# First layer's score term: copied through DRAM to all partitions in place of four TensorE transposes, with the kept products in two buffers

## The chip, the cores and the metric

The kernel runs on one core of one Trainium2 chip. The metric is the device time of one execution in microseconds, median of several runs. The engines are called as in the profile: PE is TensorE's matmul, PEld its weight load, DVE is VectorE, ACT is ScalarE, POOL is GpSimd, and SP is SyncE, whose queue (SPq) issues all DMAs of this kernel.

## What is computed

Two layers of graph attention over `x` of 64 batches x 256 nodes x 512 features, all float32. Each layer normalizes, clips at zero, attends along one 256 x 256 adjacency matrix, and adds to its input. The reference, cut to what matters:

```python
h = maximum(layernorm(x), 0)                       # layer 0
hw = h @ W                                         # 512 -> 256
e = (hw @ a[0]) + swapaxes(hw @ a[1], 1, 2)        # one term along rows, one along columns
alpha = softmax(leaky_relu(e, 0.2) + NEG * (1 - adj))
x = x + concatenate([alpha @ hw, hw], -1)

h = maximum(layernorm(x), 0)                       # layer 1: 8 heads of 64
q, k, v = h @ Wq.T + bq, h @ Wk.T + bk, h @ Wv.T + bv
attn = softmax(where(adj == 0, -inf, q k^T / 8))
x = x + (attn @ v) @ Wo.T + bo
```

In layer 0 the score of two nodes is a sum of two numbers, one for each node. The kernel holds the scores turned, with the attended node on the partitions, so one term is a number for each partition (a bias of the activation) and the other must lie along the free axis, the same on all 128 partitions. The change is about how that second term gets to all partitions.

## The kernel before, in words

A group is two batches, so there are 32 groups of 512 tokens, each in four row tiles of 128 (GT = 4). The program is unrolled; nothing loops on the chip. The main loop (lines 886 to 923) works on three groups at once: attention and output of group g (`scores`, `mask_pairs`, `weigh`, `outputs`), q, k and v of group g + 1 (`project`), and the first layer of group g + 2 (`first_layer`), with the first normalization of group g + 3 (`first_norm`) in between. These parts are generators, and two hand-written strings, `steps`, one for each batch of the group, say which of them goes on next: S is the scores, m a mask step, u a product of `project`, s a piece of `first_layer`, n a piece of `first_norm`, o an output product. PE's order is fixed to the order in which the program was written (`in_order`, line 131). Operations marked `not_sooner` stay behind their engine's last one; for the rest, the framework's scheduler chooses each engine's order when the program is built, and the engine then runs in that order. In the same way SP issues its DMAs in one fixed order, and each waits for its own semaphores while those behind it stand.

`first_layer(g)` (line 536): four products `ph` of the normalized input with W, to which two columns are joined that hold W a[1] and W a[0]. So H, 258 columns of them copied from PSUM by ACT, holds the score terms in its columns 0 and 1 and the product from column 2 on. Then `pn` (lines 551 to 553): column 0 of each of the four row tiles, read 128 times over, is transposed on PE against the identity. That leaves the 512 numbers along the free axis on every partition, in one PSUM bank. ACT then forms the scores `e` of both batches, 128 x 256 at a time, from `pn` and the bias in H's column 1; DVE does the leaky ReLU in place; ACT the exponential; and later, DVE the mask. `po` (line 577) multiplies `e` by H, and DVE divides and adds (`ri`, `x`).

`scores` (line 718): eight `sc` products of one batch, a PSUM bank each, with ACT's exponential into `p` (256 keys x 256 queries for 8 heads). `weigh` (line 754): the sums over keys (`total`), DVE's reciprocals `r`, the weighted values `pr`, and DVE's `oT` = pr times r. The `o_sums` and `sums` are operands of a seven-product scheme of matrix multiplication; `project` makes its seven products in two held banks and one turning bank. ACT copies three intermediate results out, the kept products (`kept`, line 683), to which DVE adds later products.

PSUM has five turning banks (`mm`, line 109), which `ph`, `pn`, `total`, `pr`, `sc`, `po`, second products of `project`, and products of `outputs` take in turn, and three held ones. `xt`, `passed` and `moved` (lines 443 to 462) are the normalized tiles on their way through DVE's 32 x 32 transpose and DRAM into `hT`, which is the transposed operand for the products; `passed` is stored by one DMA and `moved` fetched by four.

Of the kernel before, what the change touches and what calls it, by code (L numbers as in the profile page):

```python
# [8 lines left out]
F32 = mybir.dt.float32  # L9
I32 = mybir.dt.int32  # L10
# [4 lines left out]
P = 128  # L15
# [42 lines left out]
def bounded(  # L58
# [23 lines left out]
    nc = tc.nc  # L82
# [3 lines left out]
    B, N, D = x.shape  # L86
# [3 lines left out]
    NT = N // P  # L90
    GB = 2
    GT = GB * NT
    TOK = GB * N
# [8 lines left out]
    att = ctx.enter_context(tc.tile_pool(name="att", bufs=2))  # L102
    small = ctx.enter_context(tc.tile_pool(name="small", bufs=6))
    psum = ctx.enter_context(tc.tile_pool(name="psum", bufs=1, space=bass.MemoryType.PSUM))
    dram = ctx.enter_context(tc.tile_pool(name="dram", bufs=4, space=bass.MemoryType.DRAM))
# [3 lines left out]
    def mm(name):  # L109
        return psum.tile([P, 512], F32, tag="turn", name=name, bufs=5)  # L110
# [12 lines left out]
    def not_sooner(engine, operation, *args, **kwargs):  # L123

        last = engine.last
        after(getattr(engine, operation)(*args, **kwargs), last)
# [4 lines left out]
    def in_order(instruction):  # L131
        if before:
            after(instruction, before.pop())
        before.append(instruction.ins.name)

    def matmul(*args, **kwargs):
        in_order(nc.tensor.matmul(*args, **kwargs))  # L137

    def transpose(*args):
        in_order(nc.tensor.transpose(*args))  # L140
# [17 lines left out]
    ident = const.tile([P, P], F32, name="ident")  # L158
# [7 lines left out]

    w0_sb = const.tile([P, HP, F1 + 2], F32, name="w0_sb")
    nc.sync.dma_start(w0_sb[:, :, 2:], w0.rearrange("(c p) o -> p c o", p=P))
    adj_i = att.tile([P, NT, N], I32, tag="kept", name="adj_i", bufs=3)
    nc.sync.dma_start(adj_i, adj.rearrange("(t p) k -> p t k", p=P))  # L170

    def score_columns():
# [6 lines left out]
                )  # L179

    def mask():
        edge = att.tile([P, NT, N], F32, tag="kept", name="edge", bufs=3)
        not_sooner(vector, "tensor_scalar", edge, adj_i, 0.0, None, op0=ALU.not_equal)
        yield
        pt = mm("pt_mask").rearrange("p (k q) -> p k q", k=NT)
        for kb in range(NT):
            for t in range(NT):
                transpose(
                    pt[:, kb, t * P : (t + 1) * P], edge[:, t, kb * P : (kb + 1) * P], ident
                )  # L190
        not_sooner(vector, "tensor_copy", maskT, pt)

        not_sooner(vector, "reduce_max", bad[:, 0, :], edge, axis=AX.X)
        vector.tensor_scalar(bad[:, 0, :], bad[:, 0, :], 0.0, None, op0=ALU.is_equal)
        vector.tensor_tensor(edge, edge, adj_i, op=ALU.not_equal)
        vector.reduce_max(bad[:, 1, :], edge, axis=AX.X)
        yield
# [63 lines left out]
    def last_bias():  # L261


        wide = att.tile([P, 2, 2, P], F32, tag="kept", name="bv_wide", bufs=3)
        for q in range(NQ):
            for half in range(2):
                gpsimd.tensor_scalar(
                    wide[:, half, q, :], square_ones, bv_col[:, half, q : q + 1], None, op0=ALU.mult
                )
        yield  # L270
        pb = mm("pb")
        for q in range(NQ):
            for half in range(2):
                matmul(
                    pb, wide[:, half, q, :], w_sb["o"][:, half, 2 * q : 2 * q + 2, :],
                    start=(q == 0 and half == 0), stop=(q == NQ - 1 and half == 1),
                )
        yield
        not_sooner(vector, "tensor_add", b_out, pb, b_out)
        yield  # L280
# [116 lines left out]
    def stats(mv, src, t, name):  # L397
        st = small.tile([P, 6], F32, tag="st", name=f"st{name}_{t}", bufs=4)
        if vector.last:
            not_sooner(vector, "bn_stats", st, src[t])  # L400
        else:
            vector.bn_stats(st, src[t])
        vector.bn_aggr(mv[:, t, :], st)
# [69 lines left out]
    def operand_sums(engine, quads, sums):  # L473
        a11, a12, a21, a22 = quads
        not_sooner(engine, "tensor_add", sums[:, 0], a21, a22)
        engine.tensor_sub(sums[:, 1], sums[:, 0], a11)

        not_sooner(engine, "tensor_sub", a21, a11, a21)
        engine.tensor_sub(sums[:, 2], a12, sums[:, 1])

    def seven(quads, sums):

        a11, a12, s3, a22 = quads
        s1, s2, s4 = (sums[:, i] for i in range(3))
        return {
            1: (a11, W11), 2: (a12, W21), 3: (s4, W22), 4: (a22, T4),
            5: (s1, T1), 6: (s2, T2), 7: (s3, T3),  # L490
        }
# [41 lines left out]
    H = const.tile([P, GT, F1 + 3], F32, name="H")  # L533
    gpsimd.memset(H[:, :, F1 + 2 :], 1.0)

    def first_layer(g):

        xt = [xs[g, b][:, t, :] for b in range(GB) for t in range(NT)]
        for r in range(GT):
            b, t = divmod(r, NT)  # L540
            ph = mm(f"ph_{g}_{r}")[:, : F1 + 2]
            for c in range(HP):
                matmul(
                    ph, hT0[g, b][:, c, t * P : (t + 1) * P], w0_sb[:, c, :],
                    start=(c == 0), stop=(c == HP - 1),
                )
            scalar.copy(H[:, r, : F1 + 2], ph)
            gpsimd.tensor_add(xt[r][:, F1:], H[:, r, 2 : F1 + 2], xt[r][:, F1:])
            yield

        pn = mm(f"pn_{g}")
        for t in range(GT):
            transpose(pn[:, t * P : (t + 1) * P], H[:, t, 0:1].to_broadcast([P, P]), ident)
        pT = {}
        for b in range(GB):
            e = att.tile([P, NT, N], F32, tag="e", name=f"e_{g}_{b}")
            for kb in range(NT):
                scalar.activation(
                    e[:, kb, :], pn[:, b * N : (b + 1) * N], AF.Identity,
                    bias=H[:, b * NT + kb, 1:2], scale=1.0,  # L560
                )
            vector.scalar_tensor_tensor(e, e, ALPHA, e, op0=ALU.mult, op1=ALU.max)
            scalar.activation(e, e, AF.Exp)
            pT[b] = e
        if g:
            yield
        for b in range(GB):
            not_sooner(vector, "tensor_mul", pT[b], pT[b], maskT)
        yield
        if g == 0:  # L570
            yield
        mv = small.tile([P, GT, 2], F32, tag="mv", name=f"mv1_{g}", bufs=4)
        factors, norm, turn, fetch, put = norm_T(xt, mv, f"1_{g}", g == 0)
        row_factors = small.tile([P, GT], F32, tag="ri", name=f"ri_{g}", bufs=2)
        for r in range(GT):
            b, t = divmod(r, NT)
            po = mm(f"po_{g}_{r}")[:, : F1 + 1]
            for kb in range(NT):
                matmul(
                    po, pT[b][:, kb, t * P : (t + 1) * P], H[:, b * NT + kb, 2:],  # L580
                    start=(kb == 0), stop=(kb == NT - 1),
                )
            ri = row_factors[:, r : r + 1]
            not_sooner(vector, "reciprocal", ri, po[:, F1:])
            vector.scalar_tensor_tensor(
                xt[r][:, :F1], po[:, :F1], ri, xt[r][:, :F1], op0=ALU.mult, op1=ALU.add
            )
            stats(mv, xt, r, f"1_{g}")
            if r == 1:
                factors(0)  # L590
            elif r == 2:
                norm(0)
            elif r == 3:
                factors(1)
                if g:
                    turn(0)
                    fetch(0)
            yield
        hT = big.tile([P, HP, TOK], F32, tag="hT1", name=f"hT1_{g}")
        sums = big.tile([P, 3, 2, N], F32, tag="sums", name=f"sums_{g}", bufs=1)  # L600
        quads = [
            hT[:, 2 * c : 2 * c + 2, r * N : (r + 1) * N] for r in range(2) for c in range(2)
        ]
        operands[g] = seven(quads, sums)
        if g == 0:
            turn(0)
            put(0, hT[:, :, :N])
            yield
        norm(1)
        yield  # L610
        turn(1)
        fetch(1)
        yield
        if g:
            put(0, hT[:, :, :N])
            yield
        put(1, hT[:, :, N:])
        operand_sums(gpsimd, quads, sums)
        yield
# [18 lines left out]
    def project(g):  # L638
        ops = operands.pop(g)
        for name in ("q", "k", "v"):  # L640
# [40 lines left out]
                        after(instruction, last)  # L681

            def kept(bank, half, i):
                s = att.tile([P, 2, N], F32, tag="kept", name=f"kept{i}_{name}_{g}", bufs=3)
                take(s, bank, half)
                return s

# [195 lines left out]
    run(verdict)  # L883


    steps = ("Smmnuuuumonmuouuossnunosunosnouso", "Ssmmususuososmuomssusuonusonuouunous")
    waiting, late = None, iter(())
    for g in range(NG):
        products = project(g + 1) if g + 1 < NG else iter(())
# [404 lines left out]
```

## Time and profile before

| | before |
|---|---|
| time, median of 3 | 2510.27 us (2509.89 to 2510.88) |
| span of the profiled execution | 2506.5 us |
| granted TensorE clock | 0.999 |
| PE busy | 2473.7 us, 99% |
| DVE busy | 1684.0 us, 67% |
| ACT busy | 1009.8 us, 40% |
| POOL busy | 1018.9 us, 41% |
| DMA, mean | 82 GB/s |

The page gives busy time by engine, a row of slices over the span, the chain of work that ended last, the groups of instructions with mean duration and idle time before them, and the DMA issues. The chain follows from the last instruction back to what released each step, so it says which engine the end waits for. A group's mean duration is not its cost on PE: matmuls overlap there, so their pitch is read from the chain or from a timeline, which lists instructions in order of time with start, length and, in brackets, the idle time before and what ended it. In the steady part, the trace repeats every group.

### The profile page before, as it was taken

What the parts mean: (1) busy time and instruction counts of PE and PEld (TensorE: products, weight loads), DVE (VectorE), ACT (ScalarE), POOL (GpSimd) and SP (SyncE); (2) the same over time, 40 slices, a digit from 0 to 9 for tenths busy, and PEclk for the clock granted to TensorE, in tenths of its full rate; (3) what the DMA queues carried; (4) which work ended last, traced back from release to release, by engine and by line L of the source; (5) the groups of instructions that cost most, each with busy time, mean ns of one, the idle gap of its engine ahead of it and who ended that gap; (6) DMA issues with size and microseconds to landing.
All of it is one profiled execution on the core that took longest, in us unless ns stands there. A gap on an engine that the chain in (4) does not pass through costs nothing.

```text
span 2506.5 us, 41385 instructions
## 1 busy us (share of the span) xinstructions
PE 2473.7 (99%) x16158; PEld 2054.6 (82%) x16158; DVE 1684.0 (67%) x2971; ACT 1009.8 (40%) x2019; POOL 1018.9 (41%) x978
## 2 busy tenths in 40 slices
PE   8999999999999999999999999999999999999998
PEld 7778888888888888888888888888888888888886
DVE  6666766776667767667766667676677666676656
ACT  5533443443434434434434444344334344343321
POOL 3533434434444334444344443344443344433432
PEclk9999999999999999999999999999999999999999
DMA  5222222322232321222222323222222223232100
GB/s 189 68 85 69 67 93 81 97 74 81 73 96 82 101 74 63 92 85 93 77 84 68 101 76 102 74 69 86 85 93 84 77 68 101 76 101 75 51 28 35
DMA packets 129352, 205.39 MB, mean 82 GB/s; under 512 B 13952, under 2 KB 78208, under 8 KB 129152
## 3 DMA queue, kind: packets, MB, share of 16 engines
q1 hardware_dynamic: 129152, 202.69, 25.1%
q8 instruction: 129, 2.11, 0.4%
q14 instruction: 71, 0.58, 0.1%
HBM read 104.08 MB, written 98.57 MB: 81 GB/s over the span
## 4 chain that ended last, share of the span: by engine, by line
PE 96%; DVE 2%; DMA 1%; ACT 0%; issue 0%; POOL 0%; SPq 0%; ACTq 0%; DVEq 0%; POOLq 0%
PE pq L137 16%; PE pk L137 15%; PE py L137 15%; PE pv L137 15%; PE sc L137 10%; PE ph L137 9%; PE pr L137 8%; PE po L137 4%; PE total L137 3%; PE pn L140 1%; DMA moved<-passed 0%; DVE p L35 0%; DVE st L35 0%; DVE r L35 0%; DVE x L35 0%
## 5 line engine op out<-in xcount | busy, mean ns | idle before, releaser
L35 POOL TENSOR_TENSOR p<-p 128x512 f32<-128x512 f32 x256 | 410.2, 1617 | 688.0 <-DVE p L35 688.0
L35 DVE TENSOR_TENSOR x<-py,x 128x256 f32<-128x256 f32 x448 | 187.3, 418 | 409.5 <-PE py L137 400.8
L35 DVE TENSOR_TENSOR p<-p,maskT 128x1024 f32<-128x1024 f32 x256 | 341.3, 1354 | 0.0
L35 ACT ACTIVATE p<-sc 128x512 f32<-128x512 f32 x512 | 257.7, 624 | 195.6 <-PE sc L137 191.6
L35 ACT ACTIVATE xn<-x,factor 128x512 f32<-128x512 f32 x256 | 194.4, 807 | 202.3 <-POOL factor L35 202.3
L35 DVE RECIPROCAL r<-total 128x256 f32<-128x256 f32 x128 | 215.5, 1725 | 73.7 <-PE total L137 73.7
L137 PE MATMUL py<-wo_sb,oT 128*128 128x256 f32 x1024 | 262.4, 379 | 1.7 <-DVE x L35 1.1
L137 PE MATMUL sc<-q,k 64*128 64x256 f32 x2048 | 257.7, 389 | 0.8 <-DVE r L35 0.5
L137 PEld LDWEIGHTS sc<-q,k 64*128 64x128 f32 x2048 | 215.5, 186 | 43.5 <-issue 26.3
L137 PE MATMUL pk<-hT,wk_sb 128*128 128x256 f32 x1024 | 244.9, 382 | 0.0
L137 PE MATMUL pv<-wv_sb,hT 128*128 128x256 f32 x1024 | 238.3, 381 | 6.1 <-ACT kept_v L35 6.1
L137 PE MATMUL pq<-hT,wq_sb 128*128 128x256 f32 x1024 | 239.9, 382 | 0.0
L137 PE MATMUL ph<-w_sb,hT 128*128 128x258 f32 x1024 | 239.6, 381 | 0.3 <-ACT hT L35 0.3
L137 PE MATMUL pr<-p,v 128*32 128x256 f32 x4096 | 232.7, 379 | 0.0
L137 PEld LDWEIGHTS pv<-wv_sb,hT 128*128 128x128 f32 x1024 | 195.1, 191 | 33.5 <-ACT kept_v L35 6.9
L137 PEld LDWEIGHTS pk<-hT,wk_sb 128*128 128x128 f32 x1024 | 191.7, 190 | 36.1 <-issue 10.8
L137 PEld LDWEIGHTS pq<-hT,wq_sb 128*128 128x128 f32 x1024 | 191.8, 190 | 35.0 <-issue 9.9
L137 PEld LDWEIGHTS ph<-w_sb,hT 128*128 128x128 f32 x1024 | 194.3, 190 | 29.8 <-ACT hT L35 0.9
L137 PEld LDWEIGHTS py<-wo_sb,oT 128*128 128x128 f32 x1024 | 193.9, 190 | 29.9 <-DVE x L35 1.5
L35 POOL TENSOR_TENSOR factor<-factor,rexp 128x2 f32<-128x2 f32 x128 | 91.6, 716 | 289.8 <-DVE factor L35 289.8
L137 PEld LDWEIGHTS pr<-p,v 128*32 128x32 f32 x4096 | 133.1, 110 | 87.9
L137 PE MATMUL py<-wo_sb,o_sums 128*128 128x256 f32 x768 | 198.0, 380 | 3.6 <-DVE x L35 3.6
(122 smaller groups left out, 3665.6 us busy)
## 6 DMA issues: line engine op xcount, KB each, us to landing
passed<-xt SPq DMA_DIRECT2D x124, 512.0 KB, 2.8
moved<-passed SPq DMA_DIRECT2D x496, 128.0 KB, 3.2
x<-in_x_dram SPq DMA_DIRECT2D x64, 512.0 KB, 4.3
out_dram<-x SPq DMA_DIRECT2D x64, 512.0 KB, 3.1
wq_sb<-in_L_gnn_Wq_dram SPq DMA_DIRECT2D x2, 512.0 KB, 9.4
wk_sb<-in_L_gnn_Wk_dram SPq DMA_DIRECT2D x2, 512.0 KB, 10.7
wv_sb<-in_L_gnn_Wv_dram SPq DMA_DIRECT2D x2, 512.0 KB, 7.5
wo_sb<-in_L_gnn_Wo_dram SPq DMA_DIRECT2D x8, 128.0 KB, 3.9
```

What stands on the lines that cost most here:

```text
L35: instruction = getattr(self.engine, operation)(*args, **kwargs)
L137: in_order(nc.tensor.matmul(*args, **kwargs))
L140: in_order(nc.tensor.transpose(*args))
```

## The change

From group 1 on, the term takes another way: after the fourth H copy, SP writes column 0 of the four tiles to a line of 512 numbers in DRAM (`line`), and, once it has landed, reads that line back to all 128 partitions at once (`own`, 128 x 512 in SBUF). `e` reads `own` in place of `pn`. Group 0 keeps the transposes. The aim is to take four PE instructions a group, and a PSUM bank, out of the kernel. The DMAs are issued in the step of the fourth product, one step ahead of `e`. To make room for `own`, the tag `kept` has two buffers (the pool's default) in place of three. In the second `steps` string one product of `project` stands earlier, so that `po`, which needs `e`, comes one product later.

```diff
-    adj_i = att.tile([P, NT, N], I32, tag="kept", name="adj_i", bufs=3)
+    adj_i = att.tile([P, NT, N], I32, tag="kept", name="adj_i")
...
             gpsimd.tensor_add(xt[r][:, F1:], H[:, r, 2 : F1 + 2], xt[r][:, F1:])
-            yield
-
-        pn = mm(f"pn_{g}")
-        for t in range(GT):
-            transpose(pn[:, t * P : (t + 1) * P], H[:, t, 0:1].to_broadcast([P, P]), ident)
+            if r < GT - 1:
+                yield
+
+        if g:
+            line = dram.tile([1, GT, P], F32, tag="line", name=f"line_{g}")
+            nc.sync.dma_start(line[0].rearrange("t p -> p t"), H[:, :, 0])
+            pn = att.tile([P, TOK], F32, tag="own", name=f"own_{g}", bufs=1)
+            nc.sync.dma_start(pn, line.rearrange("o t p -> o (t p)").to_broadcast([P, TOK]))
+            yield
+        else:
+            yield
+            pn = mm(f"pn_{g}")
+            for t in range(GT):
+                transpose(pn[:, t * P : (t + 1) * P], H[:, t, 0:1].to_broadcast([P, P]), ident)
...
-                s = att.tile([P, 2, N], F32, tag="kept", name=f"kept{i}_{name}_{g}", bufs=3)
+                s = att.tile([P, 2, N], F32, tag="kept", name=f"kept{i}_{name}_{g}")
...
-    steps = ("Smmnuuuumonmuouuossnunosunosnouso", "Ssmmususuososmuomssusuonusonuouunous")
+    steps = ("Smmnuuuumonmuouuossnunosunosnouso", "Ssmmuususuososmomssusuonusonuouunous")
```

The tiles `edge` and `bv_wide`, of the same tag, lose `bufs=3` in the same way.

More of the change, by code (lines that the diff above doesn't have):

```diff
@@ L181, in mask @@
     def mask():
-        edge = att.tile([P, NT, N], F32, tag="kept", name="edge", bufs=3)
+        edge = att.tile([P, NT, N], F32, tag="kept", name="edge")
         not_sooner(vector, "tensor_scalar", edge, adj_i, 0.0, None, op0=ALU.not_equal)
@@ L261, in last_bias @@
     def last_bias():
-        wide = att.tile([P, 2, 2, P], F32, tag="kept", name="bv_wide", bufs=3)
+        wide = att.tile([P, 2, 2, P], F32, tag="kept", name="bv_wide")
         for q in range(NQ):
```

## The prediction

> **What bounds the kernel now.** I read the page's busy shares first, then the chain, then what TensorE (PE) waited for, then the groups, then short stretches of the timeline in one steady group.
>
> ```profile
> PE 2473.7 (99%) x16158; PEld 2054.6 (82%) x16158; DVE 1684.0 (67%) x2971; ACT 1009.8 (40%) x2019; POOL 1018.9 (41%) x978
> PE 96%; DVE 2%; DMA 1%; ACT 0%; issue 0%; POOL 0%; SPq 0%; ACTq 0%; DVEq 0%; POOLq 0%
> ...
> L140 PE MATMUL pn<-ident,H 128*128 128x128 f32 x128 | 19.4, 273 | 0.1
> ```
>
> PE is never idle: 96% of the chain is PE, and its named waits add up to some 27 us in 2506.5 us. So any PE instruction taken away is worth its pitch, and any new wait on PE costs its full length. The pn transposes are 128 instructions, four a group. Their 273 ns overlap, so the pitch is read from the chain, where a group's four take 0.44 us:
>
> ```profile
> 1507.97 1.73 PE pk L137 x8
> 1509.70 0.44 PE pn L140 x4
> 1510.14 0.87 PE py L137 x4
> ```
>
> The chain repeats every 76.42 us (ph at 1494.96, 1571.38), one group of two batches. Two stretches of a group decide. Stage A, the scores of batch 0, first on ACT and then on PE:
>
> ```profile
> 1548.72 1.14 ACT L35 COPY hT<-moved 128x512 f32<-128x512 f32 x2
> 1549.76 1.52 ACT L35 ACTIVATE xn<-x,factor 128x512 f32<-128x512 f32 x2
> 1553.75 4.03 ACT L35 ACTIVATE p<-sc 128x512 f32<-128x512 f32 x8 [2.47 <-PE sc L137]
> 1558.53 0.84 ACT L35 ACTIVATE kept_q<-pq,bq_sb 128x256 f32<-128x256 f32 x2 [0.75 <-PE pq L137]
> ```
> ```profile
> 1552.59 3.92 PE L137 MATMUL sc<-q,k 64*128 64x256 f32 x32
> 1556.43 3.72 PE L137 MATMUL pq<-hT,wq_sb 128*128 128x256 f32 x16
> 1559.99 1.89 PE L137 MATMUL pq<-sums,wq_sb 128*128 128x256 f32 x8
> ```
>
> ACT turns over two hT copies and two xn before the scores arrive, idles 2.47 us, does eight exponentials, and copies out the first q product (kept_q) by 1559.37. The third q product (pq<-sums) accumulates in the same bank, so it needs that copy: it starts at 1559.99, with about 0.4 us to spare after its weight load. Stage B, the scores of batch 1 (PE sc from 1515.4), on DVE:
>
> ```profile
> 1511.38 1.38 DVE L35 SCALAR_TENSOR_TENSOR e<-e 128x512 f32<-128x512 f32 x2
> 1512.68 3.36 DVE L35 RECIPROCAL r<-total 128x256 f32<-128x256 f32 x2
> 1515.96 1.22 DVE L35 TENSOR_TENSOR oT<-pr,r 128x512 f32<-128x512 f32 x2
> ```
>
> The oT products free the PSUM banks that the fourth and a later sc tile take. In the chain sc takes 4.04 us here and 3.85 us in stage A, so stage B already loses about 0.2 us.
>
> [...] the trace has 273 ns, but only 0.11 us of pitch. [...] the queue's own waits agree (moved waited for passed, 205.0 us in 95 times), so line and own run one after the other. [...] so line is 512 pieces of 4 bytes. [...]
>
> **The change, part by part.** Engines run their instructions in program order, so I compared the built orders of both programs; they are alike for groups 2 to 29.
>
> (1) Removed: four transposes in 31 groups (group 0 keeps them). 31 x 0.44 = 13.6 us, all on the path.
>
> (2) Added: line (2 KB out of H's column 0) and own (a 256 KB broadcast), on SP, then e read from SBUF. H's last copy ends at 1507.52, SP issues passed at 1507.07 for 0.34 us, so line starts at about 1507.6. Prices: passed and moved take 2.5/3.1/5.2 us to landing (least, median, most), bv_col's 4-byte pieces 1.7 to 3.3 us, b_out (the same broadcast shape) 4.5 us beside other loads. Line: between 1.7 and 3.5; I take 2.5, behind passed's 512 KB. Own: between 2.5 and 4.5; I take 2.8. So own is there at 1513.0 (1511.9 to 1515.7), where the transposes let e start at 1510.47. e itself keeps its price (ACT copies from SBUF, hT, 621 ns, and from PSUM, p, 624 ns, cost the same). Queued behind the waiting SP: out_dram (before: 1511.54) and an x load, both with tens of us of room. Queued behind e on ACT: the two e exponentials and stage B's p.
>
> (3) Moved, stage B. DVE's new order is the two reciprocals, then the two e products, then oT. The reciprocals no longer stand behind e; without pn the stage comes 0.44 us earlier, at 1515.02, and the reciprocals end there too (as in stage A: total 1548.13, reciprocals from 1549.27 for 3.37 us, sc 1552.6). Then the e products, pitch 0.65 us each, 1.30; then oT's first, 0.6. It ends 1.85 us into the stage, where before it ended at 1516.59, 1.13 us in. The fourth sc tile waits for it: PE loses 0.72 us more. e must be ready on ACT by 1514.0 plus 0.9 us for two of its four pieces; own at 1513.0 is 1.0 us ahead of that, so the transfer hides behind the reciprocals. ACT's p starts 1.9 us in instead of 1.1; the fifth sc tile needs the first p by 2.7 and gets it at 2.5. Net per group 0.72 - 0.44 = +0.28; 30 groups: +8.4 us.
>
> (4) Moved, stage A. With own in front, and po and a pk product exchanged by the new steps string, batch 1's transposes xt stand later on DVE. On SP, out_dram of batch 0 now stands ahead of the four moved loads for hT, not behind. The built ACT order follows: four p, then two hT, two xn, then four p, then kept_q. Pitches from the rows above and their starts: p 0.48, hT 0.52, xn 0.72, kept_q 0.84 for both. From the first p, 1.1 us into the stage: 8 x 0.48 + 2 x 0.52 + 2 x 0.72 + 0.84 = 7.16, so kept_q ends 8.26 in. The third q product stood 7.34 in; with 0.2 us for its weight load it can now start at 8.5. PE loses 1.15 us, in each of 28 groups: 32.2 us. GpSimd's sums start after hT, 4.2 us in, and two at 1.3 us make 6.8, below 8.5, so they hide. The moved loads: out_dram issues some 5.5 us before the stage, the last moved 3.5 us before, 4 us to land, there at 0.5; hT wants it at 3.0: hidden.
>
> (5) Kept products in two buffers, not three. The third copy (kept2) must wait for DVE's addition that read the first, the next product's copies for its other additions. In q, that addition is ready 9.1 us into stage A and kept2 is due after 11: hidden by the products between. For k and v several us lie between as well: nothing.
>
> (6) Prologue: group 1's e waits for its DMA pair with little PE work in between (pb, 2 us, and two pk, 3.5 us): between 0 and 5 us, once; I take +2.5.
>
> Sum: stage B +8.4 holds 30 of the 31 savings; the last saving, -0.4. 2510.3 + 8.4 - 0.4 + 32.2 + 2.5 = 2553.0 us.
>
> **Rivals.** All hidden: PE gains 13.6 us and no wait is new: 2510.3 - 13.6 = 2496.7 us, faster. For: DVE 67%, ACT 40% busy. Against: in-order ACT has 7.16 us of work in a stage that gives it 6.0.
> Late transfer: own lands at 1515, not 1513 (b_out's 4.5 us, or slow 4-byte pieces). It passes the deadline by 1.0 us in 30 groups: 2553 + 30 = 2583 us. For: SP and the queues carry passed just then. Against: 1.0 us of room.
> Half the stage A stall: if ACT's pieces pack closer than read (0.6 us, not 1.15): 2553 - 15 = 2538 us; without stage B's loss as well, 2525.
> Two buffers bind: a wait of 0.5 us in each of three products, 31 x 1.5 = 46 us on top, 2599 us; against it the room in (5).
>
> **How the numbers follow.** As worked out (2545 to 2562): 0.58. Late transfer: 0.18. Smaller stalls, still slower: 0.10. All hidden or nearly, faster: 0.07. Losses that cancel the saving, within 0.2%: 0.03. Buffers bind: 0.04. Slower in all: 0.90. The range, 2532 to 2592, holds the first, most of the second and part of the third.
>
> **What would show it.** Right: pn only in group 0; PE waits on ACT kept_q (some 1 us, 28 times) and on DVE oT (some 0.7 us, 30 times), about 50 us together where it had none in steady state; ACT rows of p split in fours around hT and xn; the group's period 76.42 + 1.4 = 77.8 us. Wrong: PE still at 99% with a period of 75.98 (all hidden); ACT e waiting for DMA own with DVE idle behind it for long (late transfer); PE or ACT waiting for DVE's q, k or v additions (buffers).

## The result, and the profile after

| | before | changed |
|---|---|---|
| median | 2510.08 us (2509.62 to 2510.88, 4 runs) | 2895.51 us (2894.43 to 2895.71, 4 runs) |
| ratio to before | | 1.1534, 95% interval 1.1514 to 1.1554 |
| span, mean granted clock | 2506.5 us, 0.999 | 2892.8 us, 0.943 |
| one group of two batches (median) | 76.42 us | 88.73 us |

The change costs 385 us, where 43 had been predicted. These lines of the changed kernel's page answer to those shown of before: busy time with its share of the span, then the chain that ended last by engine and by line.

```profile
PE 2559.1 (88%) x16034; PEld 2089.6 (72%) x16034; DVE 1674.1 (58%) x2971; ACT 1033.5 (36%) x2019; POOL 1005.2 (35%) x978
...
PE 70%; DMA 16%; ACT 9%; DVE 2%; issue 2%; POOL 0%; SPq 0%; ACTq 0%; DVEq 0%; POOLq 0%
PE pv L137 13%; PE pk L137 11%; PE py L137 11%; DMA line<-H 10%; PE pq L137 10%; PE ph L137 8%; PE sc L137 7%; DMA own<-line 5%; PE po L137 4%; PE pr L137 4%; ACT p L35 3%; ACT e L35 2%; ACT xn L35 2%; PE total L137 1%; ACT hT L35 1%
```

Before, PE made up 96% of the chain. Now the landing of line alone is 10% of it, as much as all q products (pq). Note also that PE is busy for 85 us longer although it has 124 instructions fewer: some of them take longer than they did (the reason comes below). The next lines are from the view of waits (engine and what it waits with, what it waits for, total us, times, longest):

```profile
ACT e L35 <- DMA own<-line: 355.4, 31, 12.4
DVE e L35 <- ACT e L35: 261.6, 32, 15.7
...
PE sc L137 <- DVE oT L35: 241.4, 28, 9.6
...
PE pq L137 <- ACT kept_q L35: 25.6, 28, 0.9
```

Read from the top, they are one cascade: ACT's e waits 11.5 us a group for own, DVE's e product stands at the head of its engine meanwhile (8.16 us of idle DVE in the group below), oT is behind it and starts at 1763.35 there, although its operands were ready by 1753.8, and PE's scores need the bank that oT frees (8.6 us, 28 times). The last line is the predicted stage A wait, 0.91 us each. The chain in one steady group (start, length, what) gives the lengths:

```profile
1745.92 0.38 ACT H L35
...
1746.32 11.09 DMA line<-H
...
1757.43 3.49 DMA own<-line
...
1761.00 1.71 ACT e L35 x4
...
1763.35 0.69 DVE oT L35
...
1764.09 5.44 PE sc L137 x22
```

Line takes 11.09 us to land (9.2 us in the median, counted from its issue), own 3.49. The last line is a second loss: these 22 records of sc took 5.44 us, where stage B's whole sc took 4.04 before. The view by windows tells why. Each row has a stretch, its length, the busy time of PE, PEld, DVE, ACT and POOL in it, and at the end the granted clock, the DMA share and the GB/s:

```profile
1745.00:1754.00 9.00, 9.00 (x103) 6.23 (x103) 5.03 (x6) 1.21 (x3) 0.64 (x1) 1.00 0.18 58
1755.00:1759.00 4.00, 0.28 (x2) 0.00 (x0) 0.00 (x0) 0.00 (x0) 0.00 (x0) 1.00 0.07 25
1759.10:1769.30 10.20, 5.21 (x22) 3.85 (x22) 7.18 (x12) 6.81 (x13) 0.67 (x1) 0.50 0.34 118
1769.40:1780.00 10.60, 10.60 (x50) 9.29 (x50) 5.39 (x14) 2.68 (x6) 4.77 (x5) 1.00 0.01 2
```

PE falls idle near 1755, the clock is halved from 1759.1 to 1769.3, and so the first 5.3 us of work after the wait run at half speed. The clock records of the trace have this halving of 10.24 us 30 times, 29 of them in a row, one in each steady group.

### The profile page after: what moved, and what is told of

It reads as the page before. It is cut to its first block, busy times and chain, and to the rows that moved or that the text cites. A ratio compares the mean times of both kernels' runs of the same rounds, so it can differ in the third digit from the quotient of the medians.

```text
span 2892.8 us, 41340 instructions
## 1 busy us (share of the span) xinstructions
PE 2559.1 (88%) x16034; PEld 2089.6 (72%) x16034; DVE 1674.1 (58%) x2971; ACT 1033.5 (36%) x2019; POOL 1005.2 (35%) x978
## 4 chain that ended last, share of the span: by engine, by line
PE 70%; DMA 16%; ACT 9%; DVE 2%; issue 2%; POOL 0%; SPq 0%; ACTq 0%; DVEq 0%; POOLq 0%
PE pv L137 13%; PE pk L137 11%; PE py L137 11%; DMA line<-H 10%; PE pq L137 10%; PE ph L137 8%; PE sc L137 7%; DMA own<-line 5%; PE po L137 4%; PE pr L137 4%; ACT p L35 3%; ACT e L35 2%; ACT xn L35 2%; PE total L137 1%; ACT hT L35 1%
## 5 line engine op out<-in xcount | busy, mean ns | idle before, releaser
L35 POOL TENSOR_TENSOR p<-p 128x512 f32<-128x512 f32 x256 | 383.2, 1517 | 782.4 <-DVE p L35 780.6
L137 PE MATMUL sc<-q,k 64*128 64x256 f32 x2048 | 345.2, 472 | 262.9 <-DVE oT L35 241.4
L137 PEld LDWEIGHTS sc<-q,k 64*128 64x128 f32 x2048 | 261.7, 232 | 339.2 <-DVE oT L35 252.7
L35 DVE TENSOR_TENSOR p<-p,maskT 128x1024 f32<-128x1024 f32 x256 | 363.2, 1439 | 0.0
L35 ACT ACTIVATE p<-sc 128x512 f32<-128x512 f32 x512 | 278.7, 604 | 222.6 <-PE sc L137 222.4
L35 POOL TENSOR_TENSOR sums<-hT 128x512 f32<-128x512 f32 x32 | 56.0, 1750 | 444.8 <-ACT hT L35 428.9
L137 PE MATMUL pq<-sums,wq_sb 128*128 128x256 f32 x768 | 183.7, 382 | 26.8 <-ACT kept_q L35 25.6
## 6 DMA issues: line engine op xcount, KB each, us to landing
wk_sb<-in_L_gnn_Wk_dram SPq DMA_DIRECT2D x2, 512.0 KB, 10.7
```

Of the source, the lines that this page charges most:

```text
L35: instruction = getattr(self.engine, operation)(*args, **kwargs)
```

## The experiments

The median of before was 2509.4 to 2510.0 us beside each of these runs. Their ratios are to it.

**The parts without the transfer.** First the transposes back in, all else as changed:

```diff
-        if g:
+        if g < 0:
             line = dram.tile([1, GT, P], F32, tag="line", name=f"line_{g}")
```

> The four transposes pn are back in every group, the two kept buffers and the new steps string stay. Theory (the DMA pair alone carries the loss: line's 512 pieces of 4 bytes take 9 to 11 us to complete): the waits of 8.6 us on DVE oT and the half clock go; what stays is stage A's wait of about 0.9 us on ACT kept_q in 28 groups, so 2510 + 25 = 2535 us (2510 to 2545). Rival (two buffers or the new order of the pieces cost most of it): above 2700 us.

Measured: 2547.1 us, ratio 1.0148 (1.0131 to 1.0165), 2 us above the expected range. Then the kernel before with the new string alone:

```diff
-    steps = (..., "Ssmmususuososmuomssusuonusonuouunous")
+    steps = (..., "Ssmmuususuososmomssusuonusonuouunous")
```

> The kernel before with the new second steps string and nothing else (three kept buffers, pn by transposes). Theory: the 37 us that stayed with the transposes back come from the string alone, through ACT's order in stage A: 2545 to 2549 us, PE waiting about 0.9 us on ACT kept_q in 28 groups. Rival (the two kept buffers cost part of it): 2515 to 2540 us.

Measured: 2546.6 us, 1.0146 (1.0129 to 1.0163). The two agree within 0.5 us, so the two kept buffers cost nothing that can be measured, and the new string costs 37 us by itself. The chain of the run with the transposes back shows it in stage A:

```profile
1733.41 1.11 PE sc L137 x8
...
1736.63 1.02 ACT hT L35 x2
1737.64 1.41 ACT xn L35 x2
...
1741.00 0.74 ACT kept_q L35 x2
...
1741.88 3.69 PE pq L137 x16
```

The hT copies and xn stand among the exponentials, kept_q comes late, and the third q product starts 8.47 us into the stage, where it was 7.34 before. What is left, 2895.5 - 2547.1 = 348 us and the 13.6 us that the missing transposes should have brought, belongs to the transfer.

**Line or own?** Own reads the line of the group before, which landed long ago; e then uses another group's term.

```diff
-            nc.sync.dma_start(line[0].rearrange("t p -> p t"), H[:, :, 0])
+            written = nc.sync.dma_start(line[0].rearrange("t p -> p t"), H[:, :, 0])
+            lines[g] = line
...
-            nc.sync.dma_start(pn, line.rearrange(...)...)
+            own = nc.sync.dma_start(pn, lines[max(g - 1, 1)].rearrange(...)...)
+            after(own, written.ins.name)
```

> Line is written as in the changed kernel, but own reads the line of the group before, which has long landed, so e uses another group's score term. It takes away the wait for line and leaves own, the steps and the buffers. Theory (the landing of line's 4-byte pieces is the cost): own is there 3 to 5 us after its issue, e is in time for DVE, no wait of PE on oT above 1 us, clock 1.0 throughout; without pn, 2510 - 13.6 + 25 (stage A) + some 8 (stage B) = 2530 us (2500 to 2560). Rival (own's broadcast of 256 KB is the slow one): within 60 us of 2895.

Measured: 2894.0 us, almost as if nothing had been changed, so the expectation of my theory failed. The number of the rival came, but own's broadcast isn't slow by itself: further below, behind a line of 4 pieces, the same DMA lands in 3.5 us. The DMA issues of that run (KB, median us to landing):

```profile
own<-line SPq DMA_DIRECT2D x31, 256.0 KB, 12.7
...
line<-H SPq DMA_DIRECT2D x31, 2.0 KB, 10.7
```

Own waits for no data, is issued 0.4 us behind line, and still lands after 12.7 us. So the wait on the semaphore isn't all that costs: line's pieces hold up the DMA behind them in the queue too. In the packet records own's first 2 KB packets start right behind line's, but they trickle, one of them takes 3.05 us, and the last start 12 us later. By these records, sending the pieces isn't what is slow: in the changed kernel all of line's packets of the group shown start between 1748.02 and 1748.43, each 7 to 9 ns long, and line lands at 1757.41, 9 us after the last of them.

**How many pieces, or which?** Two ways to cut the pieces to a quarter:

```diff
+            packed = small.tile([P, GT], F32, tag="packed", name=f"packed_{g}", bufs=2)
+            gpsimd.tensor_copy(packed, H[:, :, 0])
-            nc.sync.dma_start(line[0].rearrange("t p -> p t"), H[:, :, 0])
+            nc.sync.dma_start(line[0], packed)
```

> GpSimd first packs the four columns of the term into a 128 x 4 tile, line is written as 128 pieces of 16 bytes, and e reads own in steps of 4. The same numbers reach e. Theory with a price per piece (about 9 us for 512, so about 18 ns each): line lands in 2.5 to 4.5 us and the time falls to 2540 to 2620 us. Theory with a fixed price for any small write into DRAM, whatever their number: line still about 9 us, 2850 to 2910 us. Rival (line waits in the queue behind passed): as the fixed price, 2850 to 2910 us.

```diff
             scalar.copy(H[:, r, : F1 + 2], ph)
+            if g:
+                nc.sync.dma_start(line[0, r].rearrange("(p o) -> p o", o=1), H[:, r, 0:1])
```

> Line is written in four DMAs of 128 pieces of 4 bytes, each as soon as its H tile is copied out; the total of 512 pieces stays, only the last 128 are issued where line was, behind passed. Price per piece: the last lands in 2.5 to 4.5 us, 2540 to 2620 us. Fixed price of a small write: about 9 us, 2850 to 2910 us. Rival (behind passed in the queue): 2850 to 2910 us, since the last quarter stands behind passed as before.

Measured: 2629.0 us with 128 pieces of 16 bytes (a little above the range; line 1.5 us in the median), but 2814.1 us with 128 pieces of 4 bytes at a time. The issues of the second:

```profile
own<-line SPq DMA_DIRECT2D x31, 256.0 KB, 3.8
line<-H SPq DMA_DIRECT2D x124, 0.5 KB, 7.2
```

A quarter of the pieces takes 7.2 us where all took 9.2, and the time lies in neither expected range. So neither a price per piece nor a fixed price for a small write fits both runs, and passed isn't the cause either: three of these four DMAs aren't issued behind it. What the slow forms share is that 16 pieces fall into each 64 bytes of DRAM; the 16-byte pieces are 4 to 64 bytes. That made a new theory: pieces in one block of DRAM wait for each other.

**The spacing.** 512 pieces of 4 bytes throughout, only further apart; own reads group 1's compact line (e uses group 1's term), so that the reading side stays as it was. The diff is that for 64 bytes (16 numbers); the others have 128 and 4 in its place.

```diff
+            first = g == 1
-            line = dram.tile([1, GT, P], F32, tag="line", name=f"line_{g}")
+            line = dram.tile(
+                [1, GT, P, 1 if first else 16], F32, tag="first" if first else "line", ...
+            )
-            nc.sync.dma_start(line[0].rearrange("t p -> p t"), H[:, :, 0])
+            written = nc.sync.dma_start(line[0, :, :, 0].rearrange("t p -> p t"), H[:, :, 0])
```

> As the run in which own reads an older line (2894 us, own 12.7 us to landing), but each of line's 512 pieces of 4 bytes now goes 64 bytes from the next in DRAM, and own reads group 1's line, written the old way once; e uses group 1's term. Theory A (pieces that fall into one block of DRAM wait for each other: 16 of 4 bytes share 64 bytes, 4 of 16 bytes do, and the times to landing were about 9 and 2 to 3 us): own lands in 4 to 6 us, 2530 to 2650 us. Theory B (any piece of 4 bytes is slow, wherever it goes): own about 12 us, 2850 to 2910 us.

> The same with 512 bytes from piece to piece. Theory A with a block of 64 bytes: as at 64 bytes apart, within 15 us. Theory A with a block of up to 512 bytes: fast here (2530 to 2650 us) and slow or half-way at 64. Theory B: 2850 to 2910 us in both.

> As with 64 bytes apart (2584 us; own 4.4 us to landing) and with none (2894 us; own 12.7 us), but 16 bytes from piece to piece, so 4 pieces of 4 bytes share 64 bytes. Theory (pieces within one block of 64 bytes of DRAM are written one after the other, some 0.5 us each: 16 take 8 to 9 us, 1 takes nothing that shows): 4 take about 2 us, so own lands in 5 to 7 us and the time is 2610 to 2690 us. Rival (only touching pieces, without a gap between them, disturb each other): 2575 to 2595 us, as at 64 and 512.

| distance | pieces in 64 bytes | own, median to landing | time, ratio (interval) |
|---|---|---|---|
| 4 bytes (the run with the older line) | 16 | 12.7 us | 2894.0 us, 1.1531 (1.1512 to 1.1550) |
| 16 bytes | 4 | 5.8 us | 2657.9 us, 1.0588 (1.0570 to 1.0606) |
| 64 bytes | 1 | 4.4 us | 2583.8 us, 1.0301 (1.0283 to 1.0318) |
| 512 bytes | 1 | 4.4 us | 2583.0 us, 1.0287 (1.0270 to 1.0304) |

The issues of the run with 64 bytes, for the middle of the table:

```profile
own<-line SPq DMA_DIRECT2D x31, 256.0 KB, 4.4
...
line<-H SPq DMA_DIRECT2D x31, 2.0 KB, 3.1
```

As many pieces, of the same size, over the same queue behind the same passed: from 16 to 64 bytes only the spacing changes, and 74 us go. From 4 bytes to 64 it is 310 us; there the older line that own reads differs as well (the group before's, not group 1's). Estimated from own's times, each further piece in 64 bytes adds (5.8 - 4.4) / 3 = 0.47 us, then (12.7 - 5.8) / 12 = 0.58 us; from line's own landing (3.1, 3.9 and 10.7 us) it is 0.27, then 0.57. From 64 to 512 bytes nothing more comes, and at 16 bytes it isn't over, so if there is a block, it is larger than 16 bytes and no larger than 64; 32 bytes apart wasn't tried. That the pieces of a block are written one after the other fits these numbers, but isn't shown, nor is what the memory does inside; and no run tells their number in a block from the number of DMA engines that write to it. By the size of the pieces alone, all four rows would be equal.

**Only DRAM?** The pieces go into partition 0 of own in SBUF, and a second DMA copies that row to the others.

```diff
+                nc.sync.dma_start(pn[0:1, r * P : (r + 1) * P], H[:, r, 0:1])
...
+            nc.sync.dma_start(pn[1:], pn[0:1, None, :].to_broadcast([1, P - 1, TOK]))
```

> No DRAM: the 4-byte pieces of each H tile go into partition 0 of own (four DMAs of 128, as in the run with line written tile by tile, 2814 us), and a second DMA copies that row to the other 127 partitions. Theory (the slow thing is a 4-byte write into DRAM): the last 128 pieces land in 2 to 4 us, 2540 to 2640 us. Rival (any 4-byte piece is slow, also into SBUF; or they wait behind passed): about 2814 us.

Measured: 2899.2 us, in neither of the ways expected. In the chain the last 128 pieces took 2.44 us and the copy 12.09. Its packets stood at 82 ns from one to the next, 127 of them, which makes 10.4 us one after the other. That a DMA to another number of partitions would have more of them under way at once was a guess. So the same in two DMAs:

```diff
-            nc.sync.dma_start(pn[1:], pn[0:1, None, :].to_broadcast([1, P - 1, TOK]))
+            nc.sync.dma_start(pn[1:113], pn[0:1, None, :].to_broadcast([1, 112, TOK]))
+            nc.sync.dma_start(pn[113:], pn[0:1, None, :].to_broadcast([1, 15, TOK]))
```

> As the run with the row in partition 0 of own (2899 us), but the second copy goes out as two DMAs, to 112 and to 15 partitions, not as one to 127. Theory (that copy's 12.1 us came from its 127 packets going one after another, and 4-byte pieces into SBUF do not hold each other up): the pair lands in 2 to 4 us after pieces of 2.4 to 2.8 us, 2560 to 2640 us. Rival (reading one partition's row 127 times is itself slow): 2850 to 2900 us.

Measured: 2868.6 us, 1.1426 (1.1407 to 1.1445), in the range of the rival. The issues:

```profile
own<-own SPq DMA_DIRECT2D x31, 224.0 KB, 10.7
own<-H SPq DMA_DIRECT2D x124, 0.5 KB, 1.9
...
own<-own SPq DMA_DIRECT2D x31, 30.0 KB, 10.8
```

One limit had hidden another. In the packet records some 14 packets are now under way at once, but most of them take 1.07 us where 0.08 was enough one at a time, so a row of one partition is still given out at only 254 KB in 10.8 us. But the line in the middle is what was asked: touching 4-byte pieces land in 1.9 us in SBUF, in 7.2 us in DRAM.

**The half clock.** PE gets work that nobody reads in front of the scores of batch 1, in the time in which it would stand still:

```diff
+                if b == 1 and g + 2 < NG:
+                    warm = held_bank(2, f"warm_{g}")[:, :N]
+                    for i in range(32):
+                        matmul(warm, ident, maskT[:, 0, :], start=True, stop=True)
```

> The changed kernel with 32 matmuls of 128x256 that nobody reads in front of the scores of batch 1, 6.9 us at 0.216 us each (pk: 8 in 1.73 us), in the time in which PE otherwise stands still for 8.6 us. Theory (2.6 us of each group's loss is the clock at 0.5 for 10.24 us after that idle time): granted clock 0.99 or more and about 30 x 2.6 = 78 us less than 2895, 2810 to 2825 us, although PE has 213 us more to do. Rival (the half clock costs nothing or comes for another reason): 2890 to 2900 us or more.

Measured: 2962.7 us. I had misread the chain: x8 counts records, and each of these matmuls is two (64 for the 32 in the chain), so the filling took 14.0 us, more than there was to fill. With half of it:

> The changed kernel with 16 matmuls of 128x256 that nobody reads, not 32, in front of the scores of batch 1. The run with 32 showed that each is two records of 0.219 us, so that the 32 took 14.0 us, more than the idle time they were to fill; 16 take 7.0 us. PE would stand still for some 1.6 to 2 us instead of 8.6. Theory (2.6 us of each group's loss is the clock at 0.5 for 10.24 us after the long idle time): granted clock 0.99, sc in 4 us and not 5.4 beside the rest of the wait, 2810 to 2830 us with 217 us more of PE work. Rival (no such cost): 2890 to 2900 us.

Measured: 2826.0 us, 1.1263 (1.1245 to 1.1282). The windows around the wait in one group (columns as above), and the chain's sc after it:

```profile
1717.00:1723.00 6.00, 6.00 (x46) 4.78 (x39) 1.26 (x1) 0.00 (x0) 0.00 (x0) 1.00 0.05 5
1723.00:1734.00 11.00, 9.43 (x57) 7.65 (x56) 7.54 (x12) 7.58 (x16) 1.02 (x1) 1.00 0.40 119
```
```profile
1721.84 3.43 DMA own<-line
...
1725.35 1.71 ACT e L35 x4
...
1728.43 2.85 PE sc L137 x22
```

More work, 69.5 us less: the transfer is as late as ever, but at a granted clock of 1.00 sc takes 2.85 us, and not 5.44 as at 0.50. That part of the loss was the clock.

The clock records show one thing more. In the changed kernel the halvings of the steady groups begin 88.75 us apart, which is 26 times 3.413 us (the length of the one halving inside before's span, at 166.8 us), and so they do in the run with the older line and in the first with the row in SBUF. All three have a group of 88.7 us, although their e starts at different times, 11.5, 10.4 and 11.8 us after batch 1's total (medians). With line written tile by tile, most halvings lie 25 times 3.413 us apart. My guess from these numbers is that the time of a group with such a wait is drawn to a whole number of these steps, so that the equal times of the changed kernel and the run with the older line hide that e started 1.1 us earlier in the second. No run tested this by itself.

**The orders with a punctual own.** Line is cut to one partition's 4 pieces, and own reads group 1's line:

```diff
+            rows = P if first else 1
+            written = nc.sync.dma_start(line[0, :, :rows].rearrange("t p -> p t"), H[:rows, :, 0])
```

> Line is cut to 4 pieces (one partition's column), and own reads group 1's line, so e uses group 1's term; the steps string, the buffers and own's place behind passed stay. It is the transfer that the prediction reckoned with: own lands 3 to 4 us after its issue. If steps (3) and (4) are sized right, with 37 us for the string as measured: 2510 - 13.6 + 37 + 8.4 + 2.5 = 2544 us (2535 to 2556). If stage B's order on DVE costs more than 0.3 us net a group even with a punctual own (the run with pieces 64 bytes apart lost 1.7 us more than the transposes' kernel): 2565 to 2590 us.

Measured: 2569.0 us, 1.0243 (1.0226 to 1.0260). Own lands in 3.5 us. DVE's order in this build is not the one of the prediction: one reciprocal, the e products, the other reciprocal, then oT; PE waits 0.3 us a group for the second reciprocal. In the chain:

```profile
1673.59 1.11 PE sc L137 x8
...
1751.44 1.11 PE sc L137 x8
```

From stage A to stage A 77.85 us (77.78 in the median), where the prediction's sum gave 77.8. The time lies above the 2544 of the expectation, in the range that stood there for a dearer stage B, but the period shows no such loss. Most of the difference is the start, where group 1 still writes its 512 pieces: the third run of total, at 177.6 us with the transposes back, is at 192.4 here (201.4 in the changed kernel, 172.6 before).

**A form that gains.** The old string; each batch's term goes out by itself, in pieces of 8 bytes, batch 0's right after its two H tiles; batch 1's e is put behind the scores' exponentials on ACT (e_sums) and behind oT, just ahead of po, on DVE (e_exp).

```diff
+        def own_term(b):
+            gpsimd.tensor_copy(packed, H[:, tiles, 0])
+            nc.sync.dma_start(line[0], packed)
+            nc.sync.dma_start(own, line.rearrange("o p t -> o (p t)").to_broadcast([P, N]))
...
+            if g and t == NT - 1:
+                own_term(b)
...
+        if g:
+            yield
+            e_sums(1)
...
+            if g and r == 0:
+                e_exp(1)
```

> Candidate: the old steps string; the term goes out for each batch by itself, as 128 pieces of 8 bytes (GpSimd packs two columns), batch 0's right after its two H tiles; batch 1's e is formed on ACT after the scores' exponentials, and its DVE product after the oT products. Theory (the transfer costs nothing where no PE bank waits behind it): all of it hides, 2510 - 13.6 = 2497 us (2492 to 2512). Rival (8 pieces share 64 bytes, line still takes 4 to 5 us, and SP or e of batch 0 comes late all the same): 2515 to 2600 us.

Measured: 2497.3 us (2495.1 to 2499.2), 0.9946 (0.9929 to 0.9962): faster than both kernels, by a mere 0.5% of before, with the interval below 1. From its timeline:

```profile
1731.49 0.32 SPq L546 DMA_DIRECT2D line<-packed  x1
...
1735.54 0.32 SPq L548 DMA_DIRECT2D own<-line  x1
...
1738.64 3.96 PE L137 MATMUL sc<-q,k 64*128 64x256 f32 x32
1739.05 1.23 DVE L35 TENSOR_TENSOR oT<-pr,r 128x512 f32<-128x512 f32 x2
1739.80 4.03 ACT L35 ACTIVATE p<-sc 128x512 f32<-128x512 f32 x8 [3.28 <-PE sc L137]
...
1743.64 1.01 ACT L35 ACTIVATE e<-own,H 128x256 f32<-128x256 f32 x2
1744.68 1.74 DVE L35 SCALAR_TENSOR_TENSOR e<-e 128x512 f32<-128x512 f32 x1
```

Batch 1's line still takes 4 us, but nothing that PE needs stands behind it: sc goes through in 3.96 us, and e, 8 us after own's issue, no longer shows a wait. A group takes 75.83 us, 0.59 less than before: the 0.44 of the transposes, and about 0.15 in stage B, where sc in the chain takes 3.88 us and not 4.04 now that oT no longer stands behind batch 1's e. The start takes back 6.3 us (third run of total at 178.9 us, 172.6 before).

## Why the prediction was wrong

It foresaw the direction, and most terms but the largest. Step by step:

**(1) The transposes, 13.6 us: fits, but no run has it alone.** The last kernel, which hides the transfer, ends at 2497.3 us, where the rival "all hidden" came to 2496.7. That they meet so closely is luck in part: a larger gain in each group and a loss at the start nearly cancel.

**(2) Line and own: the step that failed.** It said "Line: between 1.7 and 3.5; I take 2.5" and had own there 5.4 us after line's issue, 1.0 us ahead of its deadline. Line measured 9.2 us in the median, 11.09 in the group shown, and own was there 14.6 us after line's issue, 8.2 us past the deadline. The count of pieces (512 of 4 bytes) was right; their price was not. It came from bv_col's 4-byte pieces and from passed and moved, but bv_col's go into SBUF, and 128 touching 4-byte pieces into SBUF do land in 1.9 us. No DMA of the kernel before wrote touching 4-byte pieces into DRAM, so no row of its profile had this price, and the upper bound of 3.5 us did not hold. So PE waited 8.6 us in 28 groups, where the sum had no wait for own at all.

**(3) Stage B, +0.28 us a group: the size fits, once own is punctual; its working isn't tested.** The cut line gives a period of 77.78 us against 77.62 with the transposes back, so +0.16, but DVE's order there was another than the predicted one. That the period came out at the predicted 77.8 us is thus luck in part. In the changed kernel the predicted order was there, and with own late, the e products ahead of oT are what carried its whole lateness to PE. The rival "late transfer" had this mechanism, and named its sign; it allowed 1 us where 8 came.

**(4) Stage A, 32.2 us: right.** 37 us with the string alone, 1.20 us a group against 1.15, by the place of the third q product (8.47 us against 8.5 predicted). It is the string and not own in front that does it; the prediction had named both.

**(5) Two buffers, nothing: right,** within 0.5 us.

**(6) Prologue, +2.5 us: too small.** The changed kernel is 28.8 us behind when the third run of total begins, 23.8 of them behind the run with the transposes back. The price in (2) is a part of it, but with pieces of 16 bytes, where line is quick, the start is still 13.3 us behind that run (190.9 us); the cause of that part stays open.

**Left out altogether: the clock.** Here a PE that waited nearly 9 us got half the clock for 10.24 us; about 70 us of the 385. The rival "late transfer" charged lateness one to one.

The sum by group: 8.6 (oT) + 2.6 (clock) + 1.2 (stage A) - 0.4 (pn) = 12.0 of the 12.3 us measured; without the clock's term it is 85.8 us for a group, and the run with 16 matmuls more has 85.86.

One sum of a rival doesn't come out of its terms: half the stage A stall without stage B's loss is 2538 - 8.4 = 2530 us, or 2516 with the saving of 0.44 us a group kept, not 2525.

## What to carry to other kernels

Price a DMA by a row of the same direction and the same pattern at its destination. In these runs the time of 4-byte pieces in DRAM went with their number in 64 bytes; packing them (128 pieces of 16 bytes in 1.5 us) or setting them 64 bytes apart (3.1 us) helped, and the DMA queued behind them waited as well (12.7 us to landing, where it took 3.5 behind 4 pieces). When a transfer may come late, look at what stands behind its reader on each engine: here oT stood behind e, and PE waited 8.6 us a group. The form that gained still has a line of 4 us, but its reader stands behind the work that frees PE's banks. And a change in a hand-written order is a change of its own: here one letter moved in a string cost 37 us, nearly three times what the change could bring.

## What was not expected of the hardware

- 4-byte pieces that share 64 bytes of DRAM: some 0.3 to 0.6 us for each further one (estimate from three spacings); 512 of them 64 bytes apart land in 3.1 us, touching in 9.2 to 10.7, 9 us after the last of their packets had started in the group shown, and they hold up a following DMA that doesn't depend on them (12.7 us to landing, where it took 3.5 behind 4 pieces).
- Touching 4-byte pieces into one SBUF partition: 1.9 us for 128. A row of one partition copied to 127 others: 12.1 us in one DMA, 10.8 in two; the same row out of DRAM to 128 partitions: 3.5 us.
- After an idle time of nearly 9 us (8.81 in the group shown) the clock stood at 0.5 for 10.24 us, 5.3 of them after PE had work again; with waits of 3.2 us at most (pieces of 16 bytes) the half clock came in some groups only, mostly for 3.41 us, with a mean granted clock of 0.985. In the changed kernel the halvings of the steady groups came 26 times 3.413 us apart, and a group took as long. The halvings inside the two spans, of before and of the changed kernel, last 3.413, 6.827, 10.240 (30 of them) and 13.653 us: one, two, three and four times 3.413. What sets that length, and from what it is counted, wasn't shown.
